# A fused graph layer and mixture-of-experts layer on one core: the lead-in of the experts' pipeline written out by hand, and one pipeline depth to the last row tile

## The chip, the cores and the metric

The kernel runs on one core of one Trainium2 chip. A core has five engines that each work through their own instruction queue in order and meet only at semaphores: TensorE (PE) multiplies matrices, VectorE (DVE), ScalarE (ACT) and GpSimd (POOL) do element-wise work, and SyncE (SP) issues transfers. POOL also issues the indirect transfers, those whose row addresses come from a list. All transfers run on 16 DMA engines.

The metric is the device time of one launch in microseconds (us). Three runs of the kernel before gave 2101.8, 2106.37 and 2107.72 us; the median is 2106.37 us.

## What is computed

There are 6250 nodes with 512 features each. In the first part every node averages the normalized rows of its neighbours (106250 edges), two 512x512 products and a normalization over all nodes follow, and the result is added to the node's row. In the second part every node's row ("token") goes to two of eight experts, each a small three-layer network, and the two results are added, weighted:

```python
x = x + _L0_gnn_ref(_layernorm(x), edge_index, W_l, b_l, W_r, gamma, beta)
# inside, for the second part:
logits = gelu(t @ Wg1 + bg1) @ Wg2 + bg2
topv, topi = top_k(softmax(logits), 2); topv = topv / sum(topv)
h = gelu(_ln(t @ W1[e] + b1[e]) * g1[e] + be1[e])      # 512 -> 256
h = gelu(_ln(h @ W2[e] + b2[e]) * g2[e] + be2[e])      # 256 -> 256
o = h @ W3[e] + b3[e]                                  # 256 -> 512
x = x + sum over the two experts of weight * o
```

The reference computes every expert for every token; the kernel computes only the two that are chosen, so it sorts rows by expert first. All data are float32.

## The kernel before

The first part (up to L672) gathers neighbours by indirect transfers, multiplies, sums the moments of all nodes and ends by writing the scale and shift of the normalization into the tiles `bn_a` and `bn_b`. The change does not touch it.

The second part works on 49 token tiles of 128 rows in seven groups of seven (`groups`). A token tile passes through eight small functions:

- `token_load`: two transfers bring the row and its unnormalized graph result (`xt`, `dt`).
- `token_scale` (two DVE operations, L750 and L751) and `token_shift` (one ACT operation, L756).
- `token_sum`: one DVE operation (L762), a store of the row to the output, and the row's statistics on DVE (L712, L713); `Step.scales` adds the epsilon on DVE (L722) and raises to the power -0.5 on POOL (L723).
- `Step.shifts` (DVE, L727), then `token_norm` (ACT, L732) writes the normalized row into the group's buffer `t2s`.
- `token_turn`: four PE transposes (L774) and an ACT copy (L776).
- `token_gate`: four PE products (L783) and a Gelu on ACT (L785).
- `token_logits`: one PE product (L792).

When a group's seven tiles have their logits, `route` works out, in parts separated by `yield`, which two experts each row takes and to which row of the sorted array `xs_d` it goes. `begin(q)` starts it and `part(q)` does the next piece, nearly all small DVE operations. The first seven parts (`MATH`) give the positions; then `send(q, j)` scatters a token tile into `xs_d` with two indirect transfers from POOL (L796). The last parts, `listed_all(q)`, list for the sorted row tiles ("jobs") which expert each one has. Seven of the jobs are safe to start when group 0 is listed, fourteen more with every further group, and 25 after the last: 102 jobs run.

A job passes through a pipeline with one step (`run`) per job: in step s job s is transposed (`job_turn`, L1005, L1007), job s-1 has its first layer (`layer`, PE L1015, then DVE L1018, L712, L713), s-2 is normalized (`layer_norm`, ACT), s-3 transposed with a Gelu (`layer_turn`, L1032, L1035), s-4 has its second layer, s-5 and s-6 the same two stages again, s-7 its last product (`job_product`, L1044), s-8 its bias and weight (`job_bias`, DVE L1051; `job_weigh`, ACT L1055), and s-9 its result is added to the output by an indirect accumulating transfer from POOL (`job_out`, L1059). Two such additions may meet in a row, so each waits until the one before has landed. `job_load` (SP, L990) brings a job's rows up to four steps ahead, and waits for the scatters of its group.

The order of all this is written out by hand; within an engine it is the order of the Python calls. Three pieces of that order matter here.

**The lead-in.** Before the first job, `move()` pushes one token tile per call into a line of eight places: tile i is loaded in call i, scaled two calls later, summed after three, normalized after four, turned after five, gated after six, and has its logits after seven. Fourteen calls carry group 0 to its logits, then come the seven parts of its route, then seven more calls with the sends of group 0 and its listing between them; after that the token tiles of groups 0 and 1 are done, and those of group 2 are all loaded. Five parts of group 1's route follow.

**The steps.** In `run`, with `moves` set, the same line of eight places goes on beside the jobs. For group q, `do` and `late` say in which step the parts of the route of group q+1, its sends and its listing come: for q = 0 two parts in the first step, sends in steps 1 to 4, the listing in step 5; for later groups the parts in steps 0 to 3, sends in steps 4 to 10, the listing in step 11. The position in a step is the same everywhere: token scale and sum come before `shifts`, these before `do`, and `do` before the layers' DVE work; on POOL `job_out` comes first, then the sends, then the power of `step.scales`.

**The end.** From job 77 (`LAST`, the first job of the last group) on, the distances shrink (`lag`): from job 79 every stage comes one step earlier, from job 82 the later stages two steps earlier, and the product, its bias and its weight fall into one step. Seven steps after the last transposed job end the pipeline, ten stages having become seven or eight.

Of the kernel before, what the change touches and what calls it, by code (L numbers as in the profile page):

```python
# [9 lines left out]
F32 = mybir.dt.float32  # L10
# [18 lines left out]
def gnn_moe_kernel(ctx: ExitStack, tc: tile.TileContext, x, src, dst, wlT, b_l, wrT, gamma, beta,  # L29
# [671 lines left out]
    class Step:  # L701
# [7 lines left out]
        def stats(self, row, a):  # L709
            row = 0 if row in self.used else row  # L710
            st = sb.tile([P, 6], F32, name=f"st{row}", bufs=3)
            nc.vector.bn_stats(st, a)  # L712
            nc.vector.bn_aggr(self.mv[:, row, 0:2], st)  # L713
            self.used.append(row)
            return self.mv[:, row, 1:2], self.mv[:, row, 2:3]
# [258 lines left out]

    def send(q, j):

        for i in range(2):
            row_scatter(ROUTE[q][:, i, j:j + 1], t2s[q % 2][:, j, :])
# [89 lines left out]
    let_in = 0  # L1068
    tprev = Step()
# [4 lines left out]
    def enter():  # L1074

        n = sum(a is not None for a in seq)
        seq.append(flat[n] if n < let_in else None)

    def move():

        nonlocal tprev
        enter()
        step = Step()
        for lag, f in ((7, token_logits), (5, token_turn)):
            if at(lag):
                f(*at(lag))
        tprev.shifts()
        if at(4):
            token_norm(*at(4))
        if at(3):  # L1090
            token_sum(*at(3), step)
        if at(0):
            token_load(*at(0))
        step.scales()
        if at(2):
            token_scale(*at(2))
            token_shift(*at(2))
        if at(6):
            token_gate(*at(6))
        tprev = step  # L1100
# [11 lines left out]
    LAST = done[-2] if NQ > 1 else 0  # L1112
# [3 lines left out]
    def lag(p, k):  # L1116


        i = p - LAST
        return (1, 2, 3, 4, 5, 6, 7)[k] - (i >= 2) - (i >= 5 and k >= 3)  # L1120

    products, outs = [], []

    def run(s, prev, lo, hi, moves=False, do=(), late=()):

        nonlocal products, outs

        def on(k):
            return [p for p in range(max(lo, s - 9), min(s + 1, hi)) if p + lag(p, k) == s]

        def bias():
            for p in products:
                job_bias(p)
                weigh.append(p)
            products.clear()
# [5 lines left out]
        if lo <= s < hi:  # L1141
            job_turn(s)
        for i, k in ((0, 2), (1, 5)):
            for p in on(k):
                layer_turn(p, i)
        for p in outs:
            job_out(p)
        weigh = outs = []
        bias()
        if moves:  # L1150
            for j, f in ((7, token_logits), (5, token_turn)):
                if at(j):
                    f(*at(j))
# [7 lines left out]
        for k in (1, 4):  # L1161
            for p in on(k):
                layer_norm(p)
# [4 lines left out]
        near = s >= LAST  # L1168
        if near:
            for p in on(6):  # L1170
                job_product(p)
                products.append(p)
                bias()
        else:
            for p in weigh:
                job_weigh(p)
        for f in do:
            f()
        for i, k in ((0, 0), (1, 3)):
            for p in on(k):  # L1180
                layer(p, i, step)
        if near:
            for p in weigh:
                job_weigh(p)
        else:
            for p in on(6):
                job_product(p)
                products.append(p)
# [26 lines left out]
    with tc.manual_schedule():  # L1215

        n0 = len(groups[0])
        let(min(1, NQ - 1))
        for i in range(n0 + LAGS - 1):
            move()  # L1220
# [3 lines left out]
        if NQ > 2:  # L1224
            let(2)
        for i in range(n0):
            for j in {0: (0, 1), 1: (2, 3)}.get(i, (i + 2,)):
                if j < n0:
                    send(0, j)
            if i == 3:  # L1230
                listed_all(0)
                no = sb.tile([P, RW], F32, name="xe", bufs=4)
                nc.sync.dma_start(xs_d[SLOTS], no_tokens(no))
            if i == 5:
                loads(3)
            move()
        if NQ > 1:
            begin(1)
            for i in range(5):
                part(1)  # L1240
        prev = Step()
        for q in range(NQ):
# [5 lines left out]
            if q + 1 < NQ:  # L1248
# [5 lines left out]

                if q:
                    put(do, 0, begin, q + 1)
                    for where, i in ((do, 0), (do, 0), (late, 0), (do, 1), (do, 1), (do, 2), (do, 3)):
                        put(where, i, part, q + 1)
                    a, b = 4, 10
                else:  # L1260
                    for i in (0, 0):
                        put(do, i, part, 1)
                    a, b = 1, 4
                for j in range(g):
                    put(do, a + j * (b + 1 - a) // g, send, q + 1, j)
                put(do, b, part, q + 1)
                put(do, b + 1, listed_all, q + 1)
                if q + 2 < NQ:
                    let(q + 2)
                    moves = len(groups[q + 2]) + LAGS - 1  # L1270
                    if not q:
                        moves -= n0
                    assert moves <= n
# [4 lines left out]
        for s in range(MOST, MOST + 7):  # L1278
            prev = run(s, prev, 0, MOST)
        assert not outs and not EV  # L1280
# [42 lines left out]
```

## Time and profile before

| what | value |
|---|---|
| median of three runs | 2106.37 us |
| time of the profiled execution | 2106.04 us |
| its span, first to last instruction | 2104.3 us |
| PE, DVE, ACT, POOL busy | 90, 51, 31 and 60% of the span |
| first `token_scale` (L750) starts | 1276.44 us |
| first job transposed (L1005) | 1366.31 us |
| job 77 transposed, the first after `LAST` | 1900.37 us |
| last PE instruction ends | 2084.83 us |
| last accumulating transfer issued (L1059) | 2097.08 us |

All times inside the profile count from the start of the span; the span leaves out 1.7 us of the profiled execution's time. The kernel has three very different stages, so shares of the whole say little: until 1265 us POOL's gathers and PE work on the graph part, from 1276 us to 1366 us token tiles alone run, and from there to the end jobs, beside token tiles for the first five groups. In the lines of a timeline the columns are start, duration, engine, line, operation, tiles and shapes, and in square brackets how long the engine had been idle before and what ended that. In the lines by stretch of time they are the stretch, its length, each engine's busy time and instruction count, then the granted clock of TensorE as a share of full speed, the share of the DMA engines that was busy, and GB/s.

### The profile page before, as it was taken

To read this page: it belongs to the slowest core of one execution; us is meant where nothing else is said; L and a number is where in the kernel's file an instruction comes from. 1 tells how busy PE (TensorE), PEld (TensorE's weight loads), DVE (VectorE), ACT (ScalarE), POOL (GpSimd) and SP (SyncE) were. 2 spreads that over 40 slices of the span, in tenths; PEclk is the share of its full clock that TensorE was granted. 3 is DMA by queue.
4 is the path that set the end of the run, shared out by engine and by line. 5 is a ranking of instruction groups with operands and counts; after the bars stand their busy time and mean duration, and the time that the engine had idled before them with its cause. 6 is when DMAs were issued, how large, how long until landed. Compare 5 with 4: busy or idle time off the path is not lost. (4 is left out here: it accounts for less than half of the span.)

```text
span 2104.3 us, 23852 instructions
## 1 busy us (share of the span) xinstructions
PE 1888.5 (90%) x6266; PEld 1025.4 (49%) x6266; DVE 1082.9 (51%) x2560; ACT 661.5 (31%) x1284; POOL 1258.8 (60%) x1269
## 2 busy tenths in 40 slices
PE   6989999999999999999999995588989899988894
PEld 2444444444444444444444443366766666656662
DVE  5653334334334334333433427778787877755552
ACT  3420001001000101000100114456766767645663
POOL 1447777777777777777777761435454635463343
PEclk9999999999999999999999996589999999999998
DMA  7977777777778777888878765646666756555442
GB/s 256 301 243 227 228 229 238 228 228 237 227 227 252 253 248 253 270 268 268 256 247 260 233 182 187 217 164 169 159 182 144 205 139 177 113 149 97 77 78 38
DMA packets 177854, 429.08 MB, mean 204 GB/s; under 512 B 32148, under 2 KB 38302, under 8 KB 177298
## 3 DMA queue, kind: packets, MB, share of 16 engines
q0 software_dynamic: 94208, 285.39, 48.7%
q1 hardware_dynamic: 83110, 141.22, 20.5%
q8 instruction: 56, 0.92, 0.2%
q10 hardware_dynamic: 396, 0.87, 0.1%
q14 instruction: 84, 0.69, 0.1%
HBM read 329.12 MB, written 101.32 MB: 205 GB/s over the span
## 5 line engine op out<-in xcount | busy, mean ns | idle before, releaser
L568 POOL DMA_INDIRECT xg<-xn_d,scol x882 | 848.0, 962 | 279.3 <-DMA xg<-xn_d,scol 100.9
L571 PE MATMUL pa<-xg,sel 128*128 128x512 f32 x1764 | 846.9, 602 | 46.3 <-DMA xg<-xn_d,scol 41.6
L571 PEld LDWEIGHTS pa<-xg,sel 128*128 128x128 f32 x1764 | 320.5, 191 | 437.3 <-issue 301.4
L1059 POOL DMA_INDIRECT out<-oe,to x102 | 168.3, 1650 | 179.8 <-ACT hT L1035 43.7
L723 POOL TENSOR_TENSOR mv<-mv,mhalf 128x2 f32<-128x2 f32 (+2 forms) x122 | 106.5, 873 | 226.1 <-DVE mv L722 209.3
L1015 PE MATMUL pm<-w1s,xT 128*128 x816 | 204.3, 395 | 12.9 <-DVE hn L1018 12.9
L479 ACT ACTIVATE sq<-dt 128x512 f32<-128x512 f32 x49 | 29.5, 602 | 561.0 <-DVE dt L477 285.0
L1044 PE MATMUL po<-w3s,hT 128*128 x408 | 196.4, 604 | 8.6 <-DVE oe L1051 8.6
L383 PE MATMUL ph<-wl,xT 128*128 128x512 f32 x392 | 199.8, 592 | 0.7 <-ACT xT L378 0.7
L513 DVE TENSOR_REDUCE ss<-sel 128x128 f32<-128x2304 f32 x49 | 199.9, 4080 | 0.1
L1015 PEld LDWEIGHTS pm<-w1s,xT 128*128 128x128 f32 x816 | 155.2, 198 | 46.9 <-DVE hn L1018 16.1
L458 DVE TENSOR_SCALAR rc<-pt 128x1 f32<-128x1 f32 x49 | 7.7, 158 | 312.8 <-PE pt L537 312.8
L732 ACT ACTIVATE hn<-hn,mv 128x256 f32<-128x256 f32 x204 | 111.9, 600 | 152.3 <-DVE mv L727 152.2
L1035 ACT ACTIVATE hT<-pt,gbe 128x128 f32<-128x128 f32 x408 | 154.2, 459 | 13.5 <-PE pm L1015 9.7
L796 POOL DMA_INDIRECT xs_d<-t,pos x98 | 101.7, 1038 | 40.2 <-issue 23.6
L507 DVE TENSOR_TENSOR sel<-jrow_p,dcol 128x2304 f32<-128x2304 f32 x49 | 124.4, 2539 | 0.0
L518 ACT ACTIVATE ag<-pa,rc 128x512 f32<-128x512 f32 x49 | 33.7, 687 | 288.3 <-PE pa L571 288.3
L383 PEld LDWEIGHTS ph<-wl,xT 128*128 128x128 f32 x392 | 74.4, 190 | 94.2 <-issue 93.3
L477 DVE TENSOR_TENSOR dt<-ph,shift 128x512 f32<-128x512 f32 x25 | 17.3, 692 | 197.8 <-PE ph L383 197.8
L1015 PE MATMUL pm<-w2s,hT 128*128 x408 | 108.7, 391 | 3.5 <-DVE hn L1018 3.5
L475 DVE TENSOR_TENSOR dt<-ph,xo 128x512 f32<-128x512 f32 x24 | 16.6, 691 | 183.3 <-PE ph L383 183.3
L1044 PEld LDWEIGHTS po<-w3s,hT 128*128 128x128 f32 x408 | 74.7, 192 | 69.6 <-issue 51.1
(278 smaller groups left out, 2160.4 us busy)
## 6 DMA issues: line engine op xcount, KB each, us to landing
xe<-xs_d SPq DMA_DIRECT2D x102, 264.0 KB, 3.0
xg<-xn_d,scol POOLq DMA_INDIRECT x882, 3.7
d_d<-dt SPq DMA_DIRECT2D x49, 256.0 KB, 3.8
dt<-d_d SPq DMA_DIRECT2D x49, 256.0 KB, 4.4
xt<-in_x SPq DMA_DIRECT2D x24, 512.0 KB, 5.3
xn_d<-xt SPq DMA_DIRECT2D x24, 512.0 KB, 3.0
xt<-in_x SPq DMA_DIRECT2D x48, 256.0 KB, 3.2
out<-xt SPq DMA_DIRECT2D x48, 256.0 KB, 3.2
```

The source lines that it names most:

```text
L383: nc.tensor.matmul(p, xT[:, k, :], w[:, k, :], start=start and k == 0, stop=stop and k == KD - 1)
L507: nc.vector.tensor_tensor(SEL[t], jrow_p[:, None, :].to_broadcast([P, KS, P]), dcol[:, t // TG, (t % TG) * KS:(t % TG + 1) * KS, None].to_ ...
L513: nc.vector.tensor_reduce(ss, SEL[t].rearrange("p k j -> p j k"), AX.X, OP.add)
L568: nc.gpsimd.indirect_dma_start(out=xg, out_offset=None, in_=xn_d[:, :], in_offset=bass.IndirectOffsetOnAxis(ap=scol[:, t // TG, c:c + 1], ...
L571: nc.tensor.matmul(PA[t], SEL[t][:, k, :], xg, start=(k == 0), stop=(k == KS - 1))
L723: nc.gpsimd.tensor_tensor(self.part[:, :, 1], self.part[:, :, 1], mhalf[:, :hi - lo], op=OP.pow)
L732: nc.scalar.activation(out_, in_, AF.Identity, bias=scale_shift[1], scale=scale_shift[0])
L796: st = nc.gpsimd.indirect_dma_start(out=xs_d.rearrange("n p c -> (n p) c"), out_offset=bass.IndirectOffsetOnAxis(ap=at, axis=0), in_=rows_ ...
L1015: nc.tensor.matmul(pm, lhs[:, k, :], w[:, k, ds(e, 1), :].rearrange("p o h -> p (o h)"), start=(k == 0), stop=(k == kk - 1))
L1035: nc.scalar.activation(hT[:, k, :], pt[:, k, :], AF.Gelu, bias=gb[:, 2 * i + 1:2 * i + 2], scale=gb[:, 2 * i:2 * i + 1])
L1044: nc.tensor.matmul(po, hT[:, k, :], w3s[:, k, ds(e, 1), :].rearrange("p o h -> p (o h)"), start=(k == 0), stop=(k == KH - 1))
L1059: st = nc.gpsimd.indirect_dma_start(out=out[:, :], out_offset=bass.IndirectOffsetOnAxis(ap=to[:, 0:1], axis=0), in_=OE.pop(p), in_offset=N ...
```

## The change

The lead-in no longer uses `move()`, which is gone. A new function `ahead(i)` does, for one call, everything of token tile i at short distances: logits of i-3, scale and shift of i, `shifts` and norm of i-1, sum of i, turn of i-1, gate of i-2. Nine such calls (tiles 0 to 8) come before group 0's route, five (tiles 9 to 13) behind it, with two scatters of group 0 before each (`send_one`). The listing of group 0 and its last four scatters follow, then a piece written out by hand: it finishes group 1, sums tile 14, scales tile 15, and does the first two parts of group 1's route. Tiles 16 and 17 are loaded by then, 18 to 20 are not.

So the steps take over more: three more token tiles enter in steps 0 to 2, five parts of group 1's route move from the lead-in and step 0 into steps 1 and 2, group 1's sends go into steps 3 to 5 (six, four and four scatters), and since group 2's last tile has its logits in step 9, group 2's route starts in the fourth step of the next group (step 10 where it was step 7), its sends in steps 13 to 18 and its listing in step 19 (they were in 11 to 17 and 18). From group 3 on nothing moves.

At the end `lag`, `products` and `outs` are gone: every job keeps the distances 0 to 9, and ten steps follow the last transposed job where seven did. The line in `Step.stats` that reused a place for the statistics of two jobs in one step goes too.

```diff
+    def send_one(q, j, i):
+        row_scatter(ROUTE[q][:, i, j:j + 1], t2s[q % 2][:, j, :])
...
-    def move():
-        nonlocal tprev
-        enter()
-        step = Step()
-        for lag, f in ((7, token_logits), (5, token_turn)):
-            if at(lag):
-                f(*at(lag))
-        tprev.shifts()
...
+    def ahead(i):
+        def late_one(k, f):
+            if i >= k:
+                f(*flat[i - k])
+        if i >= 3 and flat[i - 3] in tokens:
+            token_logits(*flat[i - 3])
+        token_scale(*flat[i])
+        token_shift(*flat[i])
+        if i:
+            STEP[i - 1].shifts()
+        late_one(1, token_norm)
+        STEP[i] = Step()
+        token_sum(*flat[i], STEP[i])
+        STEP[i].scales()
+        late_one(1, token_turn)
+        late_one(2, token_gate)
...
-    LAST = done[-2] if NQ > 1 else 0
...
-    def lag(p, k):
-        i = p - LAST
-        return (1, 2, 3, 4, 5, 6, 7)[k] - (i >= 2) - (i >= 5 and k >= 3)
...
-        near = s >= LAST
-        if near:
-            for p in on(6):
-                job_product(p)
-                products.append(p)
-                bias()
...
+        if on(1):
+            layer(s - 1, 0, step)
+        if on(4):
+            layer(s - 4, 1, step)
+        if on(7):
+            job_product(s - 7)
...
-        n0 = len(groups[0])
-        let(min(1, NQ - 1))
-        for i in range(n0 + LAGS - 1):
-            move()
+        n0, n1 = len(groups[0]), len(groups[1])
+        for i in range(3):
+            token_load(*flat[i])
+        for i in range(n0 + 2):
+            ahead(i)
+            token_load(*flat[i + 3])
+            if i == 3:
+                no = sb.tile([P, RW], F32, name="xe", bufs=4)
+                nc.sync.dma_start(xs_d[SLOTS], no_tokens(no))
+        token_logits(*flat[n0 - 1])
         begin(0)
         for i in range(MATH):
             part(0)
...
+        ways = [(j, i) for j in range(n0) for i in range(2)]
+        for i in range(n0 + 2, n0 + n1):
+            for w in ways[:2]:
+                send_one(0, *w)
+            ways = ways[2:]
+            ahead(i)
+            token_load(*flat[i + 3])
+        listed_all(0)
+        for w in ways:
+            send_one(0, *w)
+        n = n0 + n1
+        token_logits(*flat[n - 3])
+        token_scale(*flat[n])
+        token_shift(*flat[n])
+        STEP[n - 1].shifts()
+        token_norm(*flat[n - 1])
+        tprev = Step()
+        token_sum(*flat[n], tprev)
+        loads(3)
+        tprev.scales()
+        token_turn(*flat[n - 1])
+        token_gate(*flat[n - 2])
+        token_load(*flat[n + 3])
+        token_scale(*flat[n + 1])
+        token_shift(*flat[n + 1])
+        token_logits(*flat[n - 2])
+        token_gate(*flat[n - 1])
+        token_logits(*flat[n - 1])
+        begin(1)
+        part(1)
+        part(1)
+        seq += [None] * n + flat[n:n + 4]
+        entered = n + 4
...
+                c = 3 if q == 1 else 0
                 if q:
-                    put(do, 0, begin, q + 1)
+                    put(do, c, begin, q + 1)
...
-                    a, b = 4, 10
+                    a, b, end = 6 if c else 4, 11 if c else 10, 12 if c else 11
                 else:
-                    for i in (0, 0):
-                        put(do, i, part, 1)
-                    a, b = 1, 4
+                    for where, i in ((late, 1), (do, 2), (do, 2), (do, 2), (do, 2)):
+                        put(where, i, part, 1)
+                    a, b, end = 3, 5, 5
...
-        for s in range(MOST, MOST + 7):
+        for s in range(MOST, MOST + 10):
             prev = run(s, prev, 0, MOST)
```

## The prediction

> **What bounds the kernel now.** I read the stretches of time first, then DVE's and POOL's timelines inside those the change touches. The graph part, up to 1265 us, is untouched; so are steps 21 to 76 of the jobs. By stretch (lead-in until group 0's route; that route; the rest of the lead-in; group 1's route; steps 0 to 6; 7 to 20; the steps after job 77):
>
> ```profile
> 1276.44:1316.60 40.16, 23.72 (x114) 15.63 (x114) 35.06 (x79) 24.43 (x40) 9.78 (x11) 0.62 0.62 207
> 1316.60:1326.31 9.71, 4.05 (x18) 2.76 (x18) 8.56 (x51) 2.59 (x5) 0.00 (x0) 0.70 0.10 39
> 1326.31:1361.44 35.13, 20.74 (x84) 13.44 (x84) 26.16 (x74) 16.55 (x27) 21.29 (x21) 0.50 0.71 244
> 1361.44:1368.51 7.07, 2.99 (x13) 2.52 (x14) 5.09 (x30) 2.49 (x5) 0.00 (x0) 0.74 0.84 299
> 1368.51:1409.75 41.24, 35.49 (x187) 26.77 (x186) 28.19 (x111) 22.41 (x45) 18.04 (x21) 0.88 0.50 170
> 1409.75:1508.50 98.75, 91.10 (x433) 63.82 (x432) 77.41 (x263) 67.13 (x141) 46.49 (x41) 0.98 0.63 166
> ...
> 1900.40:2058.20 157.80, 143.14 (x608) 99.99 (x607) 81.69 (x271) 92.13 (x203) 61.53 (x51) 0.97 0.45 78
> ```
>
> The third busy column is DVE's. It leads until step 13 or so: 35.1 of 40.2 us, 28.2 of 41.2, and steps 9 to 12 have hardly a gap. Up to step 20 the change alters no DVE operation, only where it stands; so what counts is how long DVE waits. Its waits before:
>
> ```profile
> 1298.76 0.69 DVE L762 SCALAR_TENSOR_TENSOR xt<-dt,xt 128x512 f32<-128x512 f32 x1 [0.81 <-ACT xt L756]
> ...
> 1339.38 0.16 DVE L727 SCALAR_TENSOR_TENSOR mv<-mv 128x1 f32<-128x1 f32 x1 [3.31 <-POOL mv L723]
> ...
> 1388.17 0.16 DVE L727 SCALAR_TENSOR_TENSOR mv<-mv 128x2 f32<-128x2 f32 x1 [2.79 <-POOL mv L723]
> ...
> 1393.84 0.16 DVE L727 SCALAR_TENSOR_TENSOR mv<-mv 128x1 f32<-128x1 f32 x1 [3.71 <-POOL mv L723]
> ```
>
> (The last two are steps 3 and 4: the power stands behind four scatters on POOL.) At the end POOL leads, since each accumulating transfer waits for the one before:
>
> ```profile
> 1912.50 1.60 POOL L1059 DMA_INDIRECT out<-oe,to  x1 [2.52 <-DMA out<-oe,to]
> ...
> 1939.78 1.60 POOL L1059 DMA_INDIRECT out<-oe,to  x1 [1.98 <-ACT xT L1007]
> 1947.35 0.88 POOL L723 TENSOR_TENSOR mv<-mv,mhalf 128x3 f32<-128x3 f32 x1 [5.97 <-DVE mv L722]
> 1948.43 1.59 POOL L1059 DMA_INDIRECT out<-oe,to  x1 [0.20 <-issue]
> ...
> 2076.68 1.59 POOL L1059 DMA_INDIRECT out<-oe,to  x1 [3.30 <-DMA out<-oe,to]
> 2077.74 1.16 POOL L723 TENSOR_TENSOR mv<-mv,mhalf 128x1 f32<-128x1 f32 x1
> 2082.19 1.59 POOL L1059 DMA_INDIRECT out<-oe,to  x1 [3.29 <-DMA out<-oe,to]
> ```
>
> From 1912.50 to 1939.78 five of them follow at 5.46 us; at the very end they follow at 5.51. Between, the shrinking distances put three statistics into one step (the 128x3 row), POOL waits 5.97 us for them, and the chain starves.
>
> **The change part by part.** The sum is made against the profiled execution, 2106.04 us, 0.33 us under the median of the runs shown. Times in brackets count from the first scale, 1276.44.
>
> *Tiles 0 to 8 and group 0's route.* A tile costs DVE 3.25 us (1281.22 to 1284.47, L762 to L762). Before, tiles pass at 3.25 to 4.03. With short distances one loop joins the engines: norm to turn 0.87 us, turn to gate 1.05, gate to Gelu 1.98 (1.89 of L783 and a hop of 0.09), Gelu to the next shift 0.27, shift to norm 0.71: 4.88 us per tile at the half clock, 3.58 at full clock (turn 0.59, gate 1.14). The first four tiles go as fast as before but for a Gelu table load (1.28): tile 2's norm at [13.0], tile 5's at [27.6]. The clock was at half until 1306.9 in spite of a busy PE, and I take that to hold: full from [30.5] on. Then tile 6's norm is at [32.1], 7's at [35.7], and group 0's route starts at [39.1] where it started at [40.2]: nine calls take as long as fourteen, with two tiles fewer scaled. Bounds: [42.3] at half clock throughout, [31.6] if DVE's 3.25 set the pace.
>
> *Tiles 9 to 15.* The route takes 9.7 us, to [48.8]. PE rests meanwhile, so half clock again: tile 12's norm at 50.4 + 0.9 + 4 x 4.88 less the overlap of the first, [70.0], DVE ends tile 13 at [71.8]. Two scatters per tile (2.7 us) and a power (0.9) fit into POOL's 4.88. Then in series: listing 4.7 (1342.53 to 1347.27), scale 1.4, norm 13, turn, gate 12, Gelu, gate 13 (1.89), Gelu, logits [86.0]. DVE is done with tile 15 at [81.3] and stands still 4.7 us. Two route parts (3.2) and the register load (1.2): DVE begins step 0 at [90.4], before at [92.07]: **-1.7**. But three tiles (9.8 us of DVE) and route parts of 2.6 us (6.5 in steps 1 and 2, 3.9 of which stood in step 0 before) have gone into the steps. The output stores and row loads on SP are the same in number, three tiles' later; SP's load of job 0 waits for the last scatter to land [81.7] and has the rows at [86], in time. The empty tile's memset (0.5 us of DVE) and store move into tile 3, where DVE waits anyway; POOL's wait for that store (0.88 at 1351.61) goes.
>
> *Steps 0 to 6.* Same way of counting, DVE per step: job registers 0.3 to 0.5, scale 1.33, sum 1.67, layers 1.1 each, epsilon and shift 0.3. Step 0 3.5 us; 1 5.7 (0.9 of it waiting for the first layer behind a late turn); 2 11.4 with four parts (6.5); 3 5.0; 4 10.6 with six scatters ahead of its power (1.2 waited) and a listing part (3.9); 5 6.2; 6 3.2; with gaps 46.6 instead of 41.24: **+5.4**. The 13 us that DVE stood idle there before are the cover; the two POOL waits (2.79, 3.71) shrink, since sums now come first. If all were absorbed: 0; if PE falls back to half clock: +9.
>
> *A new wait.* Group 1's last scatter issues in step 5 at [132], where it was at 1395.33 [118.9], behind two powers. Group 0's last took 5.3 us from its start to SP's next issue (1353.04 to 1358.32), then 3.0 (the profile's median to landing for `xe<-xs_d`): job 7's rows land at [140.3], DVE is ready at [137.0]: **+3.4** (0 to 5). Behind SP's waiting load stand only later loads and stores; behind job 7's transposes, first in PE's step, stands all of step 7.
>
> *Steps 7 to 20.* Steps 7 to 9 now hold gate and logits of the late tiles instead of the route: PE 7.3, 6.6, 5.5, so 19.4 where 19.3 passed. Then the route's 10 us fall on steps 10 to 12, which have scale and sum as well (7.0 us of DVE): 9.6 to 10.9 us each, and step 13 with four sends. From step 7's start to step 14's 56.5 us instead of 49.2 (1409.75 to 1458.95): **+7.3**; the listing part in step 18 and the listing in step 19, beside full PE steps, **+0.6**. Job 21's load follows in step 20, one step ahead of its use, 3 us against 5.75. Bounds 0 (DVE's 21 us of idle time there take it) to +11.
>
> *The end.* From job 68's addition (1906.80) to the last (2097.08) 190.3 us pass for 33 intervals. At one distance no step holds two jobs: PE needs 5.18 us per step (1842.20 to 1847.38), less than the chain, and the power stays behind one addition. At the drain's 5.51 for 32 intervals and the last's 4.09 (2092.99 to 2097.08) it is 180.4: **-9.9**; I take -9.6 with a hiccup. The three more steps cost nothing of their own, because the chain has as many links as before. Bounds: 5.4 gives -13, 5.72 (six additions beside sends, 1812.5 to 1846.8) -3.2.
>
> Sum: -1.7 + 5.4 + 3.4 + 7.3 + 0.6 - 9.6 = +5.4, so 2111.4 against 2106.04 and, with 0.33, 2112 against the median.
>
> **Two rules weighed.** The half clock has a row: 0.50 from 1266.00 to 1306.50 and again from 1320.60 to 1361.40, PE busy 23.35 and 24.17 of some 40 us.
>
> ```profile
> 1266.00:1306.50 40.50, 23.35 (x96) 16.47 (x96) 27.67 (x71) 18.52 (x29) 8.26 (x9) 0.50 0.59 192
> 1307.00:1320.00 13.00, 6.07 (x44) 4.47 (x45) 11.87 (x37) 8.26 (x15) 2.56 (x3) 1.00 0.54 183
> ```
>
> The Trainium skill ("TensorE: Matmul & The Clock Gate", "What's actually happening") has the gate open after about 3.4 us of sustained activity. By that the tiles would run at 3.58 us nearly from the start, and the sum would be some 12 us lower, an estimate from that page; this trace shows 41 us twice.
>
> For the additions the trace has 5.46 us from one to the next, 5.0 from issue to landing in the median. The skill's "DMA: Bandwidth & Descriptors" ("Anatomy of one DMA") gives about 2.0 us plus bytes over 436 GB/s, 2.6 us for 256 KB; by that page the end would follow PE's 5.18 and the estimate would be 10 us lower. The measured row decides.
>
> **The rivals.**
>
> *The deferred work vanishes (faster).* DVE's 13 us of idle time in steps 0 to 6 and 21 us in 7 to 20 take in what was moved; then +5.4, +7.3 and 0.6 fall away, the load still waits: 2112 - 13.3 = 2098.5. For it: before, the steps wait for POOL there. Against: waits in steps 14 to 20, where most of the later idle time lies, belong to PE and can't be used in step 10. It decides from 12 us absorbed.
>
> *The clock opens early.* Full clock for tiles 9 to 13 saves 4 x 1.3 and 2.5 in the closing chain: 2104. Against: both rows above.
>
> *Ten stages cost what they look like.* If additions are held by the steps and not by landing, the end gives nothing, or at 6.0 us a step (routes beside jobs took 6.3) +7.7: 2112 + 9.6 to 17.3 = 2121 to 2129. Against: five intervals at 5.46 with PE at 12-us steps.
>
> **How the numbers follow.** The forecast 0.48, the vanishing 0.22, the clock 0.13, the dear end 0.17. The forecast's own range, from the bounds of its terms, is 2102 to 2121; with the others 2095 to 2126 leaves out 2 in 10. What a measurement here can tell from no change is 0.3%, 6.3 us. Within it lie a third of the forecast and the early clock; slower two thirds of the forecast and the dear end; faster the vanishing: 0.22, 0.29, 0.49.
>
> **What would show it.** Right: L762 to L762 at 4.9 us under a granted clock of 0.5; the first L1005 near 1364; job 7 waiting for `xe<-xs_d` for some 3 us; steps 10 to 12 at 10 us; additions at 5.5 us to the end with no 8-us gap. Wrong, if job 21 is transposed before 1515 us, if tiles pass below 4 us, or if additions after 1950 are over 5.8 us apart.

## The result and the profile after

The changed kernel takes 2108.19 us in the median of 20 runs (2102.99 to 2113.15), the kernel before 2100.99 us in 20 runs beside them (2095.58 to 2107.72). The ratio is 1.0029, with a 95% interval from 1.0018 to 1.0040: slower by about 6 us, where the forecast's sum said 5.4. The total was met, in part by luck: some terms were too dear and one gain too large, and the errors cancelled (the section on why the prediction was right works this out).

The two profiled executions stand the other way round: 2103.47 us after, 2106.04 us before. Each is one draw from a distribution 10 to 12 us wide, one near the lower end of its runs and one near the upper. So the shares by stage have to be read from several profiles, and most of the experiments below serve for that too. The graph part, which no run changed, is the widest source: its end, the first scale of a token tile, came at 1276 to 1283 us in five profiles (the first of each kernel and the three with half transfers) and at 1435 to 1459 us in the nine others. Stages are therefore counted from that first scale, to DVE's first operation of a job (the cast of its row addresses), and to the end of the span:

| us | lead-in, to job 0 | steps 0–6 | 7–13 | 14–20 | 21–76 | job 77 to the end | sum |
|---|---|---|---|---|---|---|---|
| before | 92.1 | 41.2 | 49.2 | 49.1 | 392.6 | 203.6 | 827.8 |
| before, second profile | 90.1 | 40.1 | 49.5 | 50.2 | 392.8 | 202.4 | 825.1 |
| after | 85.2 | 47.9 | 55.2 | 48.7 | 390.8 | 196.4 | 824.2 |
| after, second profile | 90.2 | 47.8 | 55.9 | 48.8 | 390.0 | 193.8 | 826.6 |

The sums do not show the 6 us: on average they are 826.5 us before and 825.4 after. The rows are for reading single stages; the difference is taken up again behind the experiments.

By stretch of time, the first profile after (the columns are those of the same view of the kernel before): the tiles until group 0's route, the rest of the lead-in, steps 0 to 6, 7 to 13, 14 to 20, and the jobs from 77 on:

```profile
1277.50:1314.00 36.50, 18.28 (x102) 12.23 (x102) 29.11 (x69) 22.28 (x35) 7.41 (x9) 0.73 0.60 202
1314.00:1362.70 48.70, 23.84 (x106) 15.91 (x106) 34.76 (x129) 18.48 (x31) 19.54 (x20) 0.57 0.57 198
1362.70:1410.60 47.90, 36.42 (x172) 27.57 (x173) 38.81 (x141) 25.78 (x48) 18.73 (x21) 0.78 0.51 176
1410.60:1465.80 55.20, 49.20 (x219) 34.98 (x217) 42.65 (x149) 35.57 (x73) 17.79 (x15) 0.91 0.53 141
1465.80:1514.50 48.70, 48.41 (x249) 34.49 (x248) 34.56 (x113) 34.05 (x74) 29.41 (x27) 1.00 0.71 196
1905.30:2042.40 137.10, 133.62 (x589) 93.64 (x588) 81.12 (x264) 87.11 (x195) 57.32 (x50) 1.00 0.49 85
```

In steps 0 to 6 DVE's busy time went from 28.2 to 38.8 us and the stretch from 41.2 to 47.9: of 10.6 us moved in, 6.7 became time and 3.9 fell into waits. In steps 7 to 13 PE is busy for 49.2 of 55.2 us: that stretch has little left to absorb.

The tiles in DVE's timeline of the first profile after, and then of the second (one line is the sum of one tile; in the brackets DVE's wait for ACT's shift):

```profile
1285.69 0.69 DVE L761 SCALAR_TENSOR_TENSOR xt<-dt,xt 128x512 f32<-128x512 f32 x1 [0.19 <-ACT xt L755]
1290.56 0.69 DVE L761 SCALAR_TENSOR_TENSOR xt<-dt,xt 128x512 f32<-128x512 f32 x1 [1.65 <-ACT xt L755]
1295.35 0.69 DVE L761 SCALAR_TENSOR_TENSOR xt<-dt,xt 128x512 f32<-128x512 f32 x1 [0.89 <-ACT xt L755]
1298.90 0.69 DVE L761 SCALAR_TENSOR_TENSOR xt<-dt,xt 128x512 f32<-128x512 f32 x1 [0.33 <-ACT xt L755]
1302.46 0.69 DVE L761 SCALAR_TENSOR_TENSOR xt<-dt,xt 128x512 f32<-128x512 f32 x1 [0.33 <-ACT xt L755]
```

```profile
1467.15 0.69 DVE L761 SCALAR_TENSOR_TENSOR xt<-dt,xt 128x512 f32<-128x512 f32 x1 [0.88 <-ACT xt L755]
1472.00 0.69 DVE L761 SCALAR_TENSOR_TENSOR xt<-dt,xt 128x512 f32<-128x512 f32 x1 [1.63 <-ACT xt L755]
1475.58 0.69 DVE L761 SCALAR_TENSOR_TENSOR xt<-dt,xt 128x512 f32<-128x512 f32 x1 [0.36 <-ACT xt L755]
1480.43 0.69 DVE L761 SCALAR_TENSOR_TENSOR xt<-dt,xt 128x512 f32<-128x512 f32 x1 [1.63 <-ACT xt L755]
```

The loop is the one the forecast described: 4.8 us apart at half clock, 3.55 at full (the forecast had 4.88 and 3.58). What differs between the two executions is how long the clock stayed at half: in the first it opened after the fourth tile, 17 us past the first scale, in the second for single tiles only. Of the 5 us between the two lead-ins 3.9 lie in the first nine tiles (the ninth's sum starts 32.1 and 36.0 us after the first scale), nearly all the rest in the closing piece, where the first has a stretch of full clock and the second has none. Over the first 80 us both have about as much half clock, 58.2 and 59.5 us: what counts is whether it falls on tiles or on the route.

At the end the gaps of 8 us are gone. POOL's timeline after, from the middle of that stretch and from its last part:

```profile
1950.63 1.59 POOL L1062 DMA_INDIRECT out<-oe,to  x1 [3.48 <-DVE cw L1004]
1951.70 1.30 POOL L722 TENSOR_TENSOR mv<-mv,mhalf 128x2 f32<-128x2 f32 x1
1956.43 1.59 POOL L1062 DMA_INDIRECT out<-oe,to  x1 [3.42 <-DVE cw L1004]
...
2057.49 1.59 POOL L1062 DMA_INDIRECT out<-oe,to  x1 [3.10 <-DMA out<-oe,to]
...
2062.99 1.59 POOL L1062 DMA_INDIRECT out<-oe,to  x1 [3.27 <-DMA out<-oe,to]
...
2068.50 1.59 POOL L1062 DMA_INDIRECT out<-oe,to  x1 [3.29 <-DMA out<-oe,to]
```

One addition per step, 5.80 us apart in the first lines and 5.50 in the drain (behind the last transposed job). The forecast called itself wrong above 5.8 us: of the 15 intervals from 1950.63 to 2037.19 seven are above it, and their mean is 5.77. In the middle the bracket names DVE, whose copy of the weights had long been done; the wait is about as long as in the drain, where the landing of the addition before is named. Where the trace has the landing, the next addition starts 0.77 us behind it in both places (landed 1973.10, next 1973.87; landed 2062.22, next 2062.99). The run with two targets below shows that it is the landing.

### The profile page after: what moved, and what is told of

It is laid out like the page before. It is cut to its first block, busy times and chain, and to the rows that moved or that the text cites. A ratio compares the mean times of both kernels' runs of the same rounds, so it can differ in the third digit from the quotient of the medians.

```text
span 2101.7 us, 23846 instructions
## 1 busy us (share of the span) xinstructions
PE 1895.1 (90%) x6266; PEld 1030.0 (49%) x6266; DVE 1086.6 (52%) x2558; ACT 663.2 (32%) x1284; POOL 1257.5 (60%) x1268
## 5 line engine op out<-in xcount | busy, mean ns | idle before, releaser
L1062 POOL DMA_INDIRECT out<-oe,to x102 | 169.6, 1663 | 193.8 <-DVE cw L1004 48.7
L722 POOL TENSOR_TENSOR mv<-mv,mhalf 128x2 f32<-128x2 f32 (+2 forms) x121 | 111.7, 923 | 209.6 <-DVE mv L721 208.8
L1018 PE MATMUL pm<-w1s,xT 128*128 x816 | 211.8, 406 | 9.0 <-DVE hn L1021 9.0
L1047 PE MATMUL po<-w3s,hT 128*128 x408 | 198.8, 610 | 10.7 <-DVE oe L1054 10.6
L1018 PEld LDWEIGHTS pm<-w1s,xT 128*128 128x128 f32 x816 | 158.6, 205 | 31.7 <-DVE hn L1021 11.6
```

What stands on the lines that cost most here:

```text
L722: nc.gpsimd.tensor_tensor(self.part[:, :, 1], self.part[:, :, 1], mhalf[:, :hi - lo], op=OP.pow)
L1018: nc.tensor.matmul(pm, lhs[:, k, :], w[:, k, ds(e, 1), :].rearrange("p o h -> p (o h)"), start=(k == 0), stop=(k == kk - 1))
L1047: nc.tensor.matmul(po, hT[:, k, :], w3s[:, k, ds(e, 1), :].rearrange("p o h -> p (o h)"), start=(k == 0), stop=(k == KH - 1))
L1062: st = nc.gpsimd.indirect_dma_start(out=out[:, :], out_offset=bass.IndirectOffsetOnAxis(ap=to[:, 0:1], axis=0), in_=OE.pop(p), in_offset=N ...
```

## The experiments

Every ratio is to runs of the kernel before on the same chip. The runs with half transfers were on a second chip, the repeat of the end alone on a third, all others on one.

**The end alone, twice.** The kernel before with fixed distances:

```diff
-        return (1, 2, 3, 4, 5, 6, 7)[k] - (i >= 2) - (i >= 5 and k >= 3)
+        return k + 1
-        for s in range(MOST, MOST + 7):
+        for s in range(MOST, MOST + 10):
```

> The kernel before with only its end changed: every job keeps the distances 0 to 9, ten steps after the last transposed job; lead-in and steps as before. The theory (the end is paced by the landing of one accumulating transfer after the other, and the old end lets that chain starve) expects 6 to 10 us less than the kernel before, a ratio of 0.9952 to 0.9971, with additions 5.4 to 5.9 us apart from job 68 to the last. The rival (ten stages cost what they look like) expects 0 to 8 us more.

Measured: 0.9978 (0.9946 to 1.0010). From job 77 to the end 194.1 us. The direction fits, but the interval includes no change; it was run again at the end of the study:

> The ten-stage end alone once more, for a narrower interval than the first time (0.9946 to 1.001) and a second profile. The theory that the end alone gains what the profiles of before and of the first such run say (203.5 and 202.3 us against 194.1 from job 77's cast to the end) expects 8 to 9 us, a ratio of 0.9958 to 0.9962. The rival that the two profiles of the kernel before fell on a long end, and that the gain is the 2 us which the runs with the new lead-in show (195.7 against 193.8), expects 0.9985 to 0.9995. In between, at 4 to 6 us, both hold in part: the old end varies from execution to execution.

Measured: 0.9992 (0.9965 to 1.0019), and 191.3 us from job 77 to the end. By the time this is the rival's figure, and the theory's 0.9958 to 0.9962 lie just outside the interval. By the stage the new end is 8 to 12 us shorter than in the two profiles of before; by the time it gains 2 to 5 us, with intervals that reach from 12 us of gain to 4 of loss. The two do not agree, and the run of the kernel before, below, takes this up.

**The front alone.** The changed kernel with `lag`, `products`, `outs` and the seven last steps of the kernel before.

> The changed kernel with the end of the kernel before: new lead-in, deferred route parts and sends, but the shrinking distances from job 77 on. The theory (deferred work costs its DVE time, as the trace after shows up to step 21) expects 10 to 15 us more than before, a ratio of 1.005 to 1.007. The rival that the deferred work vanishes expects at most 2 us more. If the two parts add, this difference and that of the end alone give the changed kernel's 6 us.

Measured: 1.0059 (1.0037 to 1.0082), 13 us of 2262. The stages: lead-in 90.2, steps 0 to 6 47.7, 7 to 13 56.0, job 77 to the end 195.7 us. The front costs what was expected, and the rival that it vanishes falls. Against the table's first row the stages up to step 20 are 11 us longer.

**Group 2's route three steps later, alone.** In the kernel before:

```diff
+                c = 3 if q == 1 else 0
-                    put(do, 0, begin, q + 1)
+                    put(do, c, begin, q + 1)
...
-                    a, b = 4, 10
+                    a, b, end = 6 if c else 4, 11 if c else 10, 12 if c else 11
```

> The kernel before with one thing of the change: group 2's route starts in step 10 instead of step 7, its sends in steps 13 to 18, its listing in step 19. Lead-in, steps 0 to 6 and end are those of before. The theory by the sum's term for steps 7 to 13 and the listing expects up to 8 us more if the route's 10 us of DVE fall on steps that are full anyway. But here the token tiles run as early as before, so steps 7 to 9 hold less work than either kernel has: if those steps get shorter by what the later ones get longer, 0 to 2 us. The rival that the deferred work vanishes expects 0.

Measured: 0.9980 (0.9954 to 1.0006). By stretch, steps 0 to 6, 7 to 9, 10 to 13 and 14 to 20:

```profile
1526.70:1567.00 40.30, 35.31 (x187) 27.33 (x186) 28.28 (x112) 22.77 (x45) 18.11 (x21) 0.88 0.49 165
1567.00:1580.80 13.80, 13.80 (x63) 9.98 (x62) 10.46 (x34) 9.58 (x21) 4.00 (x5) 1.00 0.63 180
1580.80:1617.50 36.70, 29.21 (x126) 20.68 (x125) 32.21 (x114) 24.17 (x47) 14.37 (x11) 0.91 0.52 132
1617.50:1666.40 48.90, 47.78 (x244) 34.10 (x245) 34.72 (x113) 33.20 (x72) 29.04 (x26) 1.00 0.71 191
```

Steps 7 to 9 fall from 19.3 to 13.8 us (PE busy all the time), steps 10 to 13 rise from 29.9 to 36.7; the sum moves by 1.3 us. Here moving the route is free, because the steps it leaves get shorter. In the changed kernel they don't: the late tiles' gate and logits fill them (steps 7 to 9 take 19.6 and 20.3 us in its two profiles), so the 6 to 7 us of steps 10 to 13 stay. The late route alone does not cost them; late tiles and late route do together. Late tiles without a late route can't be had, since the route needs their logits.

**The changed kernel again.**

> The changed kernel again, for a second profile and its time beside the other parts on the same chip: 4 to 8 us over the kernel before. The profile shows which of the lead-in's numbers are properties of the kernel and which change from execution to execution: the theory expects the stretch at half clock at the start of the token tiles (27.3 us in the first profile) to come out anywhere from 27 to 41 us, with tiles 4.8 us apart inside it and 3.6 us behind it.

Measured: 1.0032 (1.0009 to 1.0056), the stages in the table. The tiles as said; half clock for 59.5 of the first 80 us from the first scale, in stretches of 30.7, 10.2 and twice 23.9.

**Idle matmuls in the lead-in.**

```diff
+    def warm(n):
+        po = ps.tile([P, D], F32, name="po")
+        for _ in range(n):
+            nc.tensor.matmul(po[:, :P], ident, ident, start=True, stop=True)
...
         late_one(2, token_gate)
+        warm(3)
```

> The changed kernel with idle matmuls on TensorE in the lead-in (identity times identity into a PSUM tile that nobody reads): 8 ahead of the first tile, 3 in every call, 10 and 14 around group 0's route, 3 in the closing piece. The theory, from the clock records of the runs so far: the clock is granted in stretches of 3.41 us, one opens at full when TensorE was busy for some 85% or more of the stretch before at half clock, and tiles pass at 4.8 us under half, 3.6 under full. So the idle matmuls should open the clock by the third tile; from the first scale to the cast of job 0 it should take 78 to 82 us where the changed kernel took 90.2 on this chip, and the time should fall by 8 to 12 us, to 0.996 to 0.999 of the kernel before. The rival that tiles are paced by something other than TensorE's clock expects 90 us again, or more for the additional matmuls, and 1.003 or above.

Measured: job 0 at 83.5 us instead of 90.2, half clock for 22.0 of the first 80 us instead of 59.5, and 0.9996 (0.9973 to 1.0020) of the kernel before: 8 us less than the changed kernel on the same chip (1.0032). The tiles from the sixth on:

```profile
1464.28 0.69 DVE L761 SCALAR_TENSOR_TENSOR xt<-dt,xt 128x512 f32<-128x512 f32 x1 [0.47 <-ACT xt L755]
1467.83 0.69 DVE L761 SCALAR_TENSOR_TENSOR xt<-dt,xt 128x512 f32<-128x512 f32 x1 [0.33 <-ACT xt L755]
1471.39 0.69 DVE L761 SCALAR_TENSOR_TENSOR xt<-dt,xt 128x512 f32<-128x512 f32 x1 [0.34 <-ACT xt L755]
1474.95 0.69 DVE L761 SCALAR_TENSOR_TENSOR xt<-dt,xt 128x512 f32<-128x512 f32 x1 [0.33 <-ACT xt L755]
```

They are 3.55 us apart; the clock is full from 5.0 us on, and the three intervals before were 4.56, 3.94 and 3.69. So TensorE's clock paces the tiles of the new lead-in; work that nobody needs makes it faster. The 8 us are the difference of two ratios, each within some 5 us, and the lead-ins are one profile each: the best draw without idle matmuls, the first profile after, has 85.2. The expected 78 to 82 us were missed; the clock fell back behind the first route and twice more from the closing piece on.

**The kernel before again.**

> The kernel before once more, for a second profile of its end. In its first profile 190.2 us passed from job 68's addition to the last; with the same end in two of the runs above it was 184.9 and 185.3. If the first profile's end was typical of that end beside the old lead-in, 190 again; if that execution had a disturbed end, 185, and the term of 9.6 us in the forecast was measured against an outlier, its true size being about 4.

Measured: 1.0000 (0.9974 to 1.0027), and 190.1 us from job 68's addition to the last: no outlier of one execution. And yet the two runs with the same end and a late route for group 2 have 184.9 and 185.3. So the old end has at least two lengths, and the shorter came in the runs with the late route for group 2. Why is open.

**Two targets.** In the changed kernel:

```diff
+        where = xn_d if p % 2 else out
         st = nc.gpsimd.indirect_dma_start(
-            out=out[:, :], out_offset=...
+            out=where[:, :], out_offset=...
```

> The changed kernel with the additions of the odd jobs going to another array of the same shape, so that each addition waits for the last but one instead of the last; half of the experts' results are left out of the output. The theory that landing paces the end expects steps at TensorE's 5.2 us there: 8 to 15 us less from job 77's cast to the end than the 194 us of the changed kernel on this chip, and steps before job 60 unchanged within 2 us. The rival that the ten-stage steps themselves pace the end expects 193 to 195 us again.

Measured: 0.9854 (0.9820 to 0.9887), 162.1 us from job 77 to the end instead of 193.8, steps 21 to 60 within 1.1 us of the changed kernel's. POOL's timeline:

```profile
2112.90 1.59 POOL L1063 DMA_INDIRECT xn_d<-oe,to  x1 [0.20 <-issue]
2117.16 0.72 POOL L722 TENSOR_TENSOR mv<-mv,mhalf 128x2 f32<-128x2 f32 x1 [2.67 <-DVE mv L721]
2118.08 1.59 POOL L1063 DMA_INDIRECT out<-oe,to  x1 [0.20 <-issue]
...
2211.68 1.54 POOL L1063 DMA_INDIRECT out<-oe,to  x1 [1.08 <-DMA out<-oe,to]
2214.51 1.54 POOL L1063 DMA_INDIRECT xn_d<-oe,to  x1 [1.28 <-DMA xn_d<-oe,to]
2217.14 1.55 POOL L1063 DMA_INDIRECT out<-oe,to  x1 [1.09 <-DMA out<-oe,to]
```

Steps at PE's 5.18 us, the additions there wait for nothing, and the drain goes at 2.6 to 2.9 us instead of 5.5. That is more than the 8 to 15 us expected, because the drain gives 20.0 of the 31.7 us (57.7 to 37.7). The chain of landings costs 32 us and the ten-stage steps do not pace the end; what ten stages cost against seven without that chain, no run shows.

**Group 1's route parts early.** `begin(1)` and all seven parts in the lead-in, none in steps 1 and 2.

> The changed kernel with all seven first parts of group 1's route in the lead-in, where five of them now stand in steps 1 and 2. The theory (steps 0 to 6 grew by 6.4 us because those five parts take some 6 to 8 us of DVE there) expects the cast of job 0 some 6 to 8 us later and steps 0 to 6 some 4 to 6 us shorter: the time is 0 to 4 us above the changed kernel's, since a part costs its whole length in the lead-in. The rival that the growth of steps 0 to 6 comes from the scatters (six, four and four ahead of the power) or the three additional tiles expects steps 0 to 6 shortened by less than 2 us and the time 4 to 8 us above.

Measured: 1.0051 (1.0026 to 1.0076). Job 0 5.8 us later, steps 0 to 6 44.8 us instead of 47.8. The 3.0 us lie between what the theory and the rival said: by the stages the parts cost in the steps half of what they cost in the lead-in, so deferring them was right (the times say the same, with intervals that overlap). Not quite half of the growth of steps 0 to 6 goes with them, and 0.8 us of that is DVE's wait for job 7's rows (see the new wait below), which is gone here, since the scatters come 5 us earlier; the rest belongs to the scatters and the three tiles, which these runs do not part.

**Two half transfers.** If the wait is what costs, two shorter chains should do without leaving anything out. From job 77 on:

```diff
+        for i in range(2):
+            st = nc.gpsimd.indirect_dma_start(
+                out=out.rearrange("n (h d) -> (n h) d", h=2),
+                out_offset=bass.IndirectOffsetOnAxis(ap=to[:, i:i + 1], axis=0),
+                in_=oe[:, i * D // 2:(i + 1) * D // 2], in_offset=None, bounds_check=2 * N - 1,
+                oob_is_err=False, compute_op=OP.add)
+            tc.declare_no_dep(st.ins, group=f"half{1 - i}", reason="the other half of the columns")
+            tc.add_to_no_dep_group(f"half{i}", st.ins)
```

with row addresses 2·to and 2·to+1 in `to`.

> The changed kernel, but from job 77 on every addition is two transfers of half the columns, ordered only against the same half of the job before: two chains side by side, each with half the bytes, 1.6 us more of POOL per job. In the trace with two target arrays TensorE's steps were 5.2 us and the stretch from job 77's cast to the end 162 us instead of 194. The theory that only the wait from one landing to the next transfer paces the end expects 162 to 172 us here and 20 to 30 us off the changed kernel's time, 0.990 to 0.995 of the kernel before. The rival that the transfers are held by their own work (rows read, added and written back one after the other) and not by the wait expects 5.5 us per job again, 190 to 200 us, the time of the changed kernel or a few us more.

Measured: 0.9956 (0.9941 to 0.9970), 177.7 us from job 77 to the end. By stretch, up to job 101 and behind it:

```profile
1911.50:2039.20 127.70, 126.00 (x583) 93.13 (x582) 81.47 (x289) 86.91 (x193) 80.04 (x64) 1.00 0.54 93
2039.20:2089.20 50.00, 27.10 (x90) 14.61 (x87) 15.41 (x44) 19.39 (x41) 34.74 (x26) 0.84 0.37 42
```

Up to job 101 127.7 us instead of 137.1, PE busy for 126.0 of them. Behind it 50.0 us instead of 59.3, but 37.7 with two targets: there POOL issues two transfers of 1.6 us and a power per job, 4.5 us from pair to pair from 2049.60 to 2063.14 with no idle time over 0.55 us, and is the pace itself; behind that two of its waits name a landing. These 12 us are most of what parts this run from the one with two targets, and the expected 162 to 172 us were missed by 6, the 0.990 to 0.995 narrowly. The rival's 5.5 us per job and 190 us fall.

**The old lead-in with the late route, the ten-stage end and the half transfers**, without and with idle matmuls:

> The lead-in and steps of the kernel before, group 2's route in step 10, the ten-stage end of the changed kernel and the two half transfers from job 77 on. If the parts add as measured (old lead-in and steps 12 to 13 us below the new ones, the late route 0 to 1 less), it is 10 to 13 us below the run with the new lead-in and two halves: 0.983 to 0.990 of the kernel before if the halves work, 0.994 to 0.997 if not. The rival that the late route only seemed free beside the old end expects 5 us less of that gain.

> The run before this one with idle matmuls in the old lead-in: 10 ahead of the first call, 1 per call, 10 and 14 around group 0's route, 6 behind the last call. The old lead-in's tiles pass at 3.25 us in either clock, DVE's pace, so the theory that the clock matters only where one loop joins the engines expects little: the cast of job 0 at 86 to 90 us from the first scale where it was 90 to 92, the time 0 to 4 us below the run before. The rival that the clock is worth as much here as in the new lead-in (6.7 us) expects 83 to 85.

Measured: 0.9916 (0.9897 to 0.9935), 2082.06 us in the median beside 2100.15, and 0.9913 (0.9893 to 0.9932). The gain over the run with the new lead-in is 8 us where 10 to 13 were expected, and 0.9916 lies above the 0.983 to 0.990; the rival, 5 us less, left 5 to 8. By the stages the gain is 14 us, so this is not decided. Idle matmuls gain nothing here: job 0 at 90.3 us in both, although half clock fell from 56.1 to 45.9 of the first 80 us. They are no clean test, for the clock was at half again from 15.8 to 26.0 us, and there they kept PE busy for 95 to 100% and tiles were 3.9 and 4.1 us apart. But the old lead-in has less to gain: its tiles are 3.25 us apart, DVE's work for one, at half clock too, until gates and logits join; then, in the first profile of before, they are 4.03 us apart at half clock and 3.36 at full, where the new one has 4.8 and 3.55. Behind the route they are 6.5 us apart, with or without idle matmuls. The first of these two is 18 us faster than the kernel before, and so some 24 us faster than the changed kernel, which was not run on that chip.

## Why the prediction was right, and where it was wrong

*Tiles and lead-in (−1.7).* Right in size: 90.2, 90.2, 90.4 and 91.1 us with the new lead-in, no idle matmuls and no early route, against 90.1 to 93.5 with the old in six profiles; the forecast had 90.4. The first profile after shows −6.9, because its clock opened early. The rival of the early clock is thus no other case but a draw of the same one, and two of the forecast's alarms (tiles below 4 us, job 21 before 1515 us: it came at 1514.2) went off through it. The step that failed is "the clock was at half until 1306.9 in spite of a busy PE, and I take that to hold": in the five profiles with this lead-in the half clock of the first tiles first ends 12 to 27 us after the first scale, not at 30.5, and the forecast's own row has PE busy for 23.35 of 40.5 us (58%).

*Steps 0 to 6 (+5.4).* 47.9 and 47.8 us where 46.6 was said: right in size. In the second profile 1.0 us of it is DVE's wait for job 7's rows, which the forecast counted in the next term; without it the stretch has 46.8, just what was said.

*The new wait (+3.4).* The mechanism is there, the size was wrong. Job 7 in PE's timeline of the first profile after, then in PE's and DVE's of the second:

```profile
1410.00 0.63 PE L1008 MATMUL pt<-identx,xe 128*128 128x128 f32 x4 [0.27 <-DMA xe<-xs_d]
```

```profile
1587.34 0.63 PE L1008 MATMUL pt<-identx,xe 128*128 128x128 f32 x4 [1.85 <-DMA xe<-xs_d]
1587.23 0.15 DVE L1003 CAST to<-xe 128x1 int32<-128x1 f32 x1 [1.03 <-DMA xe<-xs_d]
```

In the first the eight products of a first layer ahead of job 7 ran at half clock (3.20 us, in the second 1.89) and took up the wait. With PE at full clock there, in the second and in three of the runs (the front alone, idle matmuls, two half transfers), PE waits 1.8 to 1.9 us for the rows and DVE about 1.0. The step that failed is the 5.3 us from the last scatter to SP's next issue, read from group 0's last scatter. In the first profile the last scatter went at 1404.19 and SP issued the load at 1407.05, 2.9 us later, as in all six profiles with the new wait. The nearer row stood in the trace before: group 1's own last scatter, started at 1395.33, landed at 1398.08, 2.75 us later. Why group 0's last took 5.3 is not shown.

*Steps 7 to 13 (+7.3).* 55.2 and 55.9 us where 56.5 was said, steps 10 to 12 at 9.7, 8.9 and 10.5 us: right. *Steps 14 to 20 (+0.6)*: −0.4 and −1.4, no cost.

*The end (−9.6).* The new end was forecast well: 180.4 us from job 68's addition to the last, measured 180.6 to 186.2 in six profiles. The measured row (5.46 us) decided rightly against the 2.6 us that the forecast worked out from the Trainium skill ("DMA: Bandwidth & Descriptors", "Anatomy of one DMA"). The third alarm, additions over 5.8 us apart, went off for seven of 15 in the middle of the stretch; the end came at 184.6 us in that profile, 4 over the 180.4. Mis-sized was the old end: 190 us in both profiles of the kernel before, 185 in two others with the same end. By time the new end is worth 6 us beside the new front (1.0059 and 1.0032 of the kernel before) and 2 to 5 alone, each within 6 to 7 us. The stage sums point the same way: against the two profiles of the kernel before, all twelve others come out 1 to 11 us better by their sums than by their times, 6 us on average. Ends some 6 us shorter than 203 us in most runs of the kernel before would account for that; no profile of it shows one.

So the front was put at 15.0 us where it costs 13 by time and 11 by stage, and the end's gain at 9.6 where it is 2 to 6 by time; that the two errors cancelled is luck. "The deferred work vanishes" fell (1.0059 for the front alone), "ten stages cost what they look like" fell with the two targets.

## What to carry to other kernels

Deferring work into another stage cost here what the stage's leading engine had to do more, less the part that fell into its waits; count the steps that the work leaves as well, because moving it is free when they shrink. Where accumulating transfers into one array must follow each other, the wait for each landing before the next issue can be the pace of the whole pipeline; splitting the columns into two chains took half of the 32 us away at the price of POOL time. A short loop through several engines makes TensorE's clock part of every turn (4.8 against 3.55 us); with more tiles between the engines it cost less (4.03 against 3.36).

## What was not expected of the hardware

The clock moves on a fixed grid: each stretch of half or full clock in the records of the 14 profiles is a multiple of 3.41 us, but for the last of a profile, which its end cuts off. What is granted in one stretch goes mostly with PE's busy share of the stretch before. The second profile after, one line per stretch of the grid (PE's busy time first, the clock third from the end):

```profile
1463.98:1467.39 3.41, 2.62 (x12) 1.53 (x10) 2.35 (x8) 1.93 (x4) 0.54 (x1) 0.50 0.89 304
1467.39:1470.80 3.41, 2.93 (x12) 1.75 (x12) 2.84 (x7) 1.01 (x2) 0.92 (x1) 0.50 0.57 189
1470.80:1474.21 3.41, 1.88 (x15) 1.41 (x14) 2.11 (x5) 2.36 (x4) 0.30 (x1) 1.00 0.32 120
1474.21:1477.62 3.41, 2.08 (x10) 1.42 (x9) 2.92 (x8) 1.87 (x4) 0.69 (x2) 0.50 0.59 211
1477.62:1481.04 3.42, 2.21 (x10) 1.32 (x8) 1.75 (x4) 2.18 (x4) 0.79 (x1) 0.50 0.48 176
1481.04:1484.45 3.41, 2.93 (x12) 1.75 (x12) 2.48 (x7) 0.91 (x3) 0.85 (x1) 0.50 0.62 227
1484.45:1487.86 3.41, 2.02 (x14) 1.41 (x14) 1.72 (x4) 2.21 (x5) 0.54 (x1) 1.00 0.30 102
1487.86:1491.28 3.42, 0.38 (x2) 0.29 (x2) 2.36 (x11) 1.53 (x2) 0.00 (x0) 1.00 0.37 137
```

2.62 us of PE (77%) leave the clock at half, 2.93 (86%) open it; at full, 1.88 us (55%) close it again, 2.02 (59%) do not. Over the lead-ins of the 14 profiles, from the first scale to job 0: at half clock none of 171 stretches with PE busy below 82.5% opened the next, 11 of 44 between 82.5 and 85.5%, 27 of 39 above; at full clock all 30 below 50.5% closed it and 2 of 66 above 56.5%. So a busy PE is needed and not always enough: in the old lead-in with idle matmuls three stretches in a row of half clock had PE busy for 95, 100 and 100%, and only the third opened the clock. Where the grid falls against the tiles is different in each execution, and so one and the same kernel shows 27.3 us of half clock in one profile and 30.7 in the next. The Trainium skill ("TensorE: Matmul & The Clock Gate", "What's actually happening") describes such a window, about 3.4 us long and free-running; the runs agree. In the first of the forecast's 41 us "in spite of a busy PE" the share was 37 to 67% up to 1293 us, then 83% three times, and the 89% of the next stretch opened the clock. That more work on PE can open it is shown by the idle matmuls in the new lead-in; the edges are read off, the share comes from modelled ends of matmuls, and what else decides is open.
